# A two-way state-space block and a residual block on one core: the column chunks' sum made by an identity product and copied by ScalarE

## The chip, the core and the metric

The kernel runs on one core of a Trainium2 chip. The metric is the device time of one execution in microseconds, from the core's own clock. Names used below: PE is the tensor engine, DVE the vector engine, ACT the scalar engine, POOL the general engine, SP the engine that issues most DMAs. SBUF is the on-chip memory, PSUM the accumulation memory that PE writes.

## What is computed

The input `x` has 8 images of 64 channels and 128 by 128 points. Layer 0 runs a bidirectional selective scan along every row and, with other weights, along every column, averages the two, normalises by groups of channels and adds the input. Layer 1 is a residual block of two 3x3 convolutions with batch normalisation. Cut to what matters here:

```python
def mamba(seq, p):                       # seq: [sequences, 128, 64]
    xz = einsum('blc,ec->ble', seq, in_w)
    x, z = xz[..., :128], xz[..., 128:]
    x = silu(causal_conv(x, conv_w, conv_b))
    dt, Bm, Cm = split(einsum('bld,ed->ble', x, xp_w))
    delta = softplus(einsum('blr,dr->bld', dt, dt_w) + dt_b)
    # h = exp(delta*A)*h + delta*x*Bm ;  y = sum_n h*Cm + x*D   (16 states per channel)
    y = selective_scan(x, delta, A, Bm, Cm, D) * silu(z)
    return einsum('bld,cd->blc', y, out_w)

xr = run_bidir(rows of x, row params)    # 0.5 * (forward + reversed)
xc = run_bidir(columns of x, col params)
x_rec = 0.5 * (xr + xc)
x1 = silu(groupnorm(x_rec) * gn_w + gn_b) + x
out = relu(bn2(conv2(relu(bn1(conv1(x1))))) + x1)
```

## The kernel before

**Tiles.** An image lies in SBUF as `xt`, 128 partitions by 64 by 128: the upper 64 partitions hold the channels of the first 64 image rows, the lower 64 those of the last 64. The result of layer 0 before normalisation is gathered in `xp`, of the same shape. A unit of work, here called a group, is four rows or four columns: `N = 512` points, that is 4 sequences of 128. An image has 32 row groups (`o == 0`) and then 32 column groups (`o == 1`), so there are 512 groups in all, `n % 64` being the place of a group in its image.

**Steps.** A group has `UN = 16` steps: four groups of states, by two directions, by two halves of the channels. A step multiplies (`drive`, L367) the replicated `du` by the replicated B values, on DVE or, for the steps 2, 5, 9, 12 and 15 (`GPS`), on POOL; scans the result (`scan`, L375 or L377, DVE) with the decay factors that ACT wrote into PSUM just before (`decay`, L355 and L358, one step ahead); and multiplies by the C values (`weigh`, L382, POOL). PE sums the weighed states into `yp` every other step (`add_up`, L398) and replicates B for the DVE multiplies (`b_rows`, L347, into the single PSUM tile with tag `b`). The decay factors of the two halves have one PSUM tile each, so a decay can only start when the scan two steps before has read its tile.

**Order.** Everything is issued by hand, in the order of the loop `for s in range(total + UN)`, under a manual schedule; every engine and SP's queue run their own instructions in that order. While the steps of group `n` run, two other things are threaded in. The generator `prepare` builds group `n + 1` in thirteen pieces at the steps `PREP`: projection and short convolution (L235, L241), `u` (L266), `delta` (L275), `du` and `dl` written to a scratch in DRAM (L287 to L289), B and C (L299, `bd`), and the reads that replicate them over the partitions (L319). Its last piece, at step 13, is the gate's projection `zp` (L235 or L241, in the same PSUM tile `b`) and its ACT copy `sz` (L310). And group `n - 1` is finished: `gate` at step 3 (L405), `emit` at steps 12 and 13.

**Emission.** `emit` multiplies the gated `y` by the output weights into a PSUM tile `op` (L411), whose 128 partitions hold the 64 output channels twice. The factor 0.25 of the averages is in the weights. At the next step, a row group's result is copied by ACT into its place in `xp` (L417). A column group's result is added by DVE to what the rows left there, one addition for each half of the partitions (L422); its target view has a column's points 512 bytes apart. DVE then takes the statistics of the four finished columns (L425). After the last column group of an image, the same step collects the statistics, starts the normalisation and creates the generator of the first convolution; the pieces of both run beside the next image's row groups.

A tail follows: normalisation and first convolution of the last image, the second convolution, and the final sum. The constant `ident`, an identity of 128 by 128, is loaded for the preparation of the weights alone.

Of the kernel before, what the change touches and what calls it, by code (L numbers as in the profile page):

```python
# [9 lines left out]
F32 = mybir.dt.float32  # L10
# [5 lines left out]
P = 128  # L16
C = 64
W = 128
HH = W // 2
N = 512  # L20
SEQ = N // W
# [11 lines left out]
def tile_mamba2d_then_resblock(ctx: ExitStack, tc: tile.TileContext, x, par, gn, p_w, o_w, new_p, bn, cst, out):  # L33
    nc = tc.nc
# [12 lines left out]
    def load(shape, src, name):  # L47
        t = const.tile(shape, F32, name=name)
        nc.sync.dma_start(out=t, in_=src)
        return t  # L50
# [8 lines left out]

    fold = const.tile([P, 32], F32, name="fold")  # L60


    wt = []
    with tc.tile_pool(name="prep", bufs=2) as prep, tc.tile_pool(name="prep_ps", bufs=2, space=PSUM) as prep_ps:
        ident = prep.tile([P, P], F32, name="ident", bufs=1)
        nc.sync.dma_start(out=ident, in_=cst["ident"])
        iv = ident.rearrange("p (c n) -> p n c", n=4)
        nc.vector.tensor_add(fold, iv[:, 0, :], iv[:, 1, :])
        nc.vector.tensor_add(fold, fold, iv[:, 2, :])
# [1 line left out]
        for o, p in enumerate(par):  # L71
# [10 lines left out]
            for hf in range(2):  # L82
                h = slice(hf * C, (hf + 1) * C)
# [34 lines left out]
            wo = const.tile([P, 2, C], F32, name=f"wo{o}")  # L118
# [37 lines left out]
        for k, w in enumerate((w1, w2s)):  # L156
            nc.vector.memset(w, 0.0)
            for blk in range(2):
                for e in range(2):
                    for m in range(2):  # L160
                        kh = 2 * blk - e - m + 1
                        if 0 <= kh < 3:
                            nc.sync.dma_start(
                                out=w[e * C : (e + 1) * C, blk, :, m * C : (m + 1) * C],
                                in_=wacc[k * C : (k + 1) * C, 3 * kh : 3 * kh + 3, :],
# [37 lines left out]
    with ExitStack() as st:  # L203
# [10 lines left out]
        xp = big.tile([P, HH, W], F32, name="xp")  # L214
# [8 lines left out]
        def load_image(b):  # L223
            xb = x[b].rearrange("p (h w) -> p h w", w=W)
            RB = HH // 8
            for k in range(8):
                nc.sync.dma_start(out=xt[:, k * RB : (k + 1) * RB, :], in_=xb[:, k * RB : (k + 1) * RB, :])
# [115 lines left out]
        def b_rows(g, r):  # L343

            half, ng, d = where(r)
            pb = psa.tile([P, N], F32, name="pb", tag="b")
            nc.tensor.matmul(pb, wt[g["o"]]["wb"][:, P * ng : P * (ng + 1)], g["u"][:, d, :], start=True, stop=True)  # L347
            g["pb"] = pb

        def decay(g, r):  # L350

            half, ng, d = where(r)
            dA = g["dA", r] = psa.tile([P, 2, SEQ, W], F32, name=f"dA{half}")
            t, edge = (slice(1, W), 0) if d == 0 else (slice(0, W - 1), W - 1)
            nc.scalar.copy(dA[:, :, :, edge], zeros)  # L355
            dl = g["dl", half, d].rearrange("p q (s t) -> p q s t", t=W)
            for j in range(2):
                nc.scalar.activation(  # L358
                    dA[:, j, :, t], dl[:, j, :, t], AF.Exp, scale=wt[g["o"]]["A"][:, 2 * half + j, ng : ng + 1]
                )  # L360
# [46 lines left out]
        def emit(g):  # L407

            o, i, w = g["o"], g["i"], wt[g["o"]]
            op = psm.tile([P, 2, N], F32, name="op", tag="pt")[:, 0, :]  # L410
            nc.tensor.matmul(op, w["wo"].rearrange("p h c -> p (h c)"), g["y"], start=True, stop=True)  # L411
            yield
            o3 = op.rearrange("p (q t) -> p q t", t=W)
            if o == 0:
                hf, r = divmod(SEQ * i, HH)
                hs = slice(hf * C, (hf + 1) * C)
                nc.scalar.copy(xp[hs, r : r + SEQ, :], o3[hs])  # L417
            else:
                for hf in range(2):
                    hs = slice(hf * C, (hf + 1) * C)  # L420
                    v = xp[hs, :, SEQ * i : SEQ * (i + 1)].rearrange("p h w -> p w h")
                    nc.vector.tensor_add(v, o3[hs, :, hf * HH : (hf + 1) * HH], v)  # L422
                if i == 0:
                    stats[g["b"]] = small.tile([P, NCH, 6], F32, name="gst", bufs=1)
                nc.vector.bn_stats(stats[g["b"]][:, i, :], xp[:, :, SEQ * i : SEQ * (i + 1)])  # L425
            yield
# [76 lines left out]
        OUT = 12  # L503
# [5 lines left out]
        pieces, norm, conv3, output = (iter(()) for _ in range(4))  # L509

        def at(s):
            return gs[s // UN], s % UN

        def fetch(s):
            if s < total and s % UN in GPS:
                b_tile(*at(s))

        def fetch_c(s):
            if s < total and s % 4 == 0:
                g, r = at(s)  # L520
                c_rows(g, where(r)[1])

        def ahead(r):

            return 2 if r == GPS[0] else 3

        with tc.manual_schedule():
            load_image(0)
            for _ in prepare(gs[0], None):
                pass  # L530
            fetch_c(0)
            fetch_c(4)
            for s in range(7):
                fetch(s)
            decay(*at(0))
            b_rows(*at(0))
            drive(*at(0))
            for s in range(total + UN):
                n, r = divmod(s, UN)
                live = n < len(gs)  # L540
                prev = gs[n - 1] if n else None
                if r == 0:
                    for _ in pieces:
                        pass
                    pieces = prepare(gs[n + 1], gs[n]) if n + 1 < len(gs) else iter(())
                if s + 1 < total:
                    decay(*at(s + 1))
                    if (s + 1) % UN not in GPS:
                        drive(*at(s + 1))
                for k in (2, 3):  # L550
                    if s + k < total and (s + k) % UN in GPS and ahead((s + k) % UN) == k:
                        drive(*at(s + k))
                if live:
                    scan(*at(s))
                    weigh(*at(s))
                if r == LAG - 1 and prev:
                    gate(prev)
                if s == total - 1:
                    nc.scalar.activation(gs[n]["sz"], gs[n]["sz"], AF.Silu)
                if s % 2 == 0 and s + 2 < total:  # L560
                    b_rows(*at(s + 2))
                if r in CONV and n % PER > 5 or r >= CONV[0] and n % PER == 5:
                    next(conv3, None)
                if r in PREP:
                    next(pieces, None)
                if r == LAG and live:
                    skip(gs[n])
                if s % 2 == 0 and LAG <= s < total + LAG:
                    add_up(*at(s - LAG))
                if r in NORM and n % PER:  # L570
                    next(norm, None)
                fetch(s + 7)
                fetch_c(s + 3)
                if r == OUT and prev:
                    if n % PER == 5:
                        next(conv3, None)
                    output = emit(prev)
                    next(output)
                elif r == OUT + 1:
                    next(output, None)  # L580
                    if n % PER == 0 and prev:
                        for _ in conv3:
                            pass
                        norm = normalize(prev["b"], stats.pop(prev["b"]))
                        next(norm)
                        conv3 = conv1(prev["b"])
                elif r == 8 and live and n % PER == PER - 2 and gs[n]["b"] + 1 < B:
                    load_image(gs[n]["b"] + 1)

            for _ in range(2 * 5):  # L590
                next(norm)
            next(conv3)
            for _ in range(NT):
                for _ in range(2):
                    next(norm, None)
                for _ in range(5):
                    next(conv3)


    with ExitStack() as st:  # L600
# [15 lines left out]
        mean, r = pooled(small, [pps[:, 0:1], pps[:, 1:2]], mv, bmat, "bn1")  # L616
        s, t = affine(small, mean, r, bnp[0], bnp[1], "bn1")
# [3 lines left out]
        for k in range(2):  # L621
            xp = big.tile([P, HH + 1, W + 2], F32, name=f"xp{k}")
# [4 lines left out]
        for b in range(B):  # L627
            xp = xps[b % 2]
# [15 lines left out]
            for k in range(0, NT, 2):  # L644
                ps = psw.tile([P, 2, N], F32, name="cps")
                for j in range(2):
                    for kw in range(3):
                        for blk in range(2):
                            r = SEQ * (k + j) + blk
# [3 lines left out]
                                start=(kw == 0 and blk == 0), stop=(kw == 2 and blk == 1),  # L653
# [5 lines left out]
                hf, j0 = divmod(SEQ * k, HH // 2)  # L659
                for e in range(2):  # L660
                    nc.sync.dma_start(
                        out=c2v[hf, :, j0 : j0 + 2 * SEQ, e, :],
                        in_=cs[e * C : (e + 1) * C].rearrange("p (j w) -> p j w", w=W),
# [4 lines left out]
        mean, r = pooled(small, [pps[:, 2:3], pps[:, 3:4]], mv2, bmat, "bn2")  # L668
        s, t = affine(small, mean, r, bnp[2], bnp[3], "bn2")
# [71 lines left out]
```

## Time and profile before

| | us |
|---|---|
| median of 3 runs | 27648.13 |
| lowest and highest | 27644.12, 27659.78 |
| profiled execution, its own time | 27638.15 |
| its span | 27636.0 |
| busy DVE | 26018.6 |
| busy POOL | 25128.0 |
| busy PE | 19347.3 |
| busy ACT | 18349.8 |

The span is the time between the first and the last instruction that the profiler recorded. Busy times leave out the time in which an engine issues DMAs, branches or waits. In a group's line of the profile, the figure after the bar is the busy time in us, then the mean time of one instruction in ns, then how long the engine had been idle just before such instructions and what ended that. An fp32 product on PE stands in the records as two matrix instructions, so 512 emissions give 1024 of them. Times in the timeline are us from the start of the span; neighbouring instructions of one line are merged there, and their number is given after the x.

### The profile page before, as it was taken

The page shows a single profiled execution, that of the slowest core. Times are in us where ns is not written, and L with a number is a line of the kernel's source. Part 1 is how long each engine was busy: PE and PEld are TensorE (multiplying, and loading weights), DVE is VectorE, ACT ScalarE, POOL GpSimd, SP SyncE. Part 2 cuts the span into 40 slices and gives each one's busy share as a digit, 9 for nine tenths or more (in the row PEclk, how much of TensorE's full clock was granted, in tenths as well). Part 3 has the DMA queues.
Part 4 walks back from the last instruction along what each step waited for, and adds up shares of the span by engine and source line. Part 5 has one row for each costly group of instructions (what it writes and reads, how often), then busy time and mean ns, then how long its engine had stood idle before and what let it go on. Part 6 is the DMA issues. An engine that isn't in the chain of part 4 may idle for free.

```text
span 27636.0 us, 232983 instructions
## 1 busy us (share of the span) xinstructions
PE 19347.3 (70%) x65068; PEld 6675.0 (24%) x65068; DVE 26018.6 (94%) x16145; ACT 18349.8 (66%) x30638; POOL 25128.0 (91%) x10916
## 2 busy tenths in 40 slices
PE   6766677666776667766676667766677666776676
PEld 1222222222222222222222222222222222222222
DVE  8999999999999999999999999999999999999942
ACT  5766666666676666766667666666667666666632
POOL 7999999999999999999999999999999999999930
PEclk8888888888888888888888888888888888888888
DMA  5555555555555555555555555555555555555545
GB/s 177 173 173 173 177 183 180 173 174 178 185 175 173 172 182 185 175 173 170 183 185 173 174 176 178 184 171 176 175 185 182 170 176 176 186 176 171 172 141 188
DMA packets 1861563, 4871.45 MB, mean 176 GB/s; under 512 B 240272, under 2 KB 387872, under 8 KB 1844384
## 3 DMA queue, kind: packets, MB, share of 16 engines
q1 hardware_dynamic: 1839664, 4754.93, 52.8%
q10 hardware_dynamic: 15984, 68.06, 0.9%
q0 software_dynamic: 4608, 33.56, 0.3%
q8 instruction: 513, 8.40, 0.1%
q14 instruction: 794, 6.50, 0.1%
HBM read 4116.04 MB, written 738.98 MB: 176 GB/s over the span
## 4 chain that ended last, share of the span: by engine, by line
DVE 40%; issue 21%; PE 17%; DMA 10%; ACT 8%; POOL 2%; SPq 1%; DVEq 0%; POOLq 0%; ACTq 0%
DVE s L367 14%; DVE s L375 12%; DVE s L377 10%; DMA du<-dd 7%; PE pb L347 6%; ACT dA L358 4%; PE yp L398 3%; PE cps L650 2%; PE dp L273 2%; PE bp L295 2%; DVE du L287 2%; POOL s L382 1%; DVE y L405 1%; DMA bt<-bd 1%; PE cp L241 1%
## 5 line engine op out<-in xcount | busy, mean ns | idle before, releaser
L382 POOL TENSOR_TENSOR s<-s,c 128x1024 f32<-128x1024 f32 x8192 | 19121.0, 2364 | 1104.3 <-DMA c<-bd 440.6
L358 ACT ACTIVATE dA<-dl,A 128x508 f32<-128x508 f32 x16384 | 11274.9, 688 | 616.4 <-DMA dl<-dd 101.1
L347 PE MATMUL pb<-u,wb 128*128 128x512 f32 x8192 | 5419.6, 748 | 7657.6 <-DVE s L367 7313.1
L377 DVE TENSOR_TENSOR_SCAN s<-dA,s 128x1024 f32<-128x1024 f32 x4096 | 9296.2, 2280 | 52.3 <-ACT dA L358 40.5
L375 DVE TENSOR_TENSOR_SCAN s<-dA,s 128x1024 f32<-128x1024 f32 x4096 | 9287.2, 2278 | 0.0
L367 DVE TENSOR_TENSOR s<-du,pb 128x1024 f32<-128x1024 f32 x5632 | 6757.8, 1200 | 559.0 <-DMA du<-dd 452.1
L367 POOL TENSOR_TENSOR s<-du,bt 128x1024 f32<-128x1024 f32 x2560 | 6055.3, 2365 | 317.3 <-DMA bt<-bd 140.6
L355 ACT COPY dA<-zeros 128x8 f32<-128x8 f32 x8192 | 1349.0, 165 | 6360.6 <-DVE s L377 4676.1
L398 PE MATMUL yp<-s,fold 128*32 128x512 f32 x32768 | 5386.2, 671 | 5.3 <-POOL s L382 5.3
L347 PEld LDWEIGHTS pb<-u,wb 128*128 128x128 f32 x8192 | 1468.9, 216 | 10579.4 <-DVE s L367 5372.1
L235 PE MATMUL cp<-xt,wc 128*128 128x512 f32 (+3 forms) x4096 | 2063.2, 628 | 132.7 <-DMA xt<-x_h 76.0
L241 PE MATMUL cp<-xc,wc 128*128 128x256 f32 (+3 forms) x8192 | 2095.3, 401 | 0.0
L241 PEld LDWEIGHTS cp<-xc,wc 128*128 128x128 f32 x8192 | 1607.4, 202 | 1038.2 <-issue 459.6
L398 PEld LDWEIGHTS yp<-s,fold 128*32 128x32 f32 x32768 | 821.7, 115 | 3451.8 <-issue 2080.6
L295 PE MATMUL bp<-u,xpT 128*32 128x512 f32 x2048 | 1636.7, 948 | 4.8 <-ACT dl L289 4.8
L358 ACT ACT_TABLE_LOAD x1030 | 1321.5, 1283 | 20.3 <-DMA dl<-dd 2.3
L235 PEld LDWEIGHTS cp<-xt,wc 128*128 128x128 f32 x4096 | 782.2, 202 | 1469.4 <-issue 1116.2
L273 PE MATMUL dp<-u,wd 128*128 128x512 f32 x2048 | 1017.3, 621 | 1.2 <-ACT u L266 1.2
L299 ACT COPY bc<-bp 32x1024 f32<-32x1024 f32 x512 | 513.1, 1002 | 744.4 <-PE yp L398 677.0
L388 PE MATMUL yp<-u,dg 128*128 128x512 f32 x2048 | 961.9, 592 | 1.2 <-DVE y L405 1.2
L679 POOL DMA_DIRECT2D out<-cc x32 | 17.2, 537 | 975.6 <-ACT cc L678 975.6
L481 PE MATMUL cps<-strip,w 128*128 128x512 f32 x1536 | 754.4, 618 | 134.3 <-DMA strip<-x_d 128.0
(107 smaller groups left out, 10117.9 us busy)
## 6 DMA issues: line engine op xcount, KB each, us to landing
c<-bd SPq DMA_DIRECT2D x2049, 512.0 KB, 4.8
dl<-dd SPq DMA_DIRECT2D x2048, 512.0 KB, 6.5
du<-dd SPq DMA_DIRECT2D x2048, 512.0 KB, 7.4
bt<-bd SPq DMA_DIRECT2D x2560, 256.0 KB, 4.7
dd<-du SPq DMA_DIRECT2D x2048, 128.0 KB, 2.3
dd<-dl SPq DMA_DIRECT2D x2048, 128.0 KB, 2.4
bd<-bc SPq DMA_DIRECT2D x512, 128.0 KB, 5.4
c_d<-cs SPq DMA_DIRECT2D x256, 256.0 KB, 5.2
```

The costliest lines, as they stand in the source:

```text
L235: nc.tensor.matmul(ps[:, :, lo:hi], lhsT[hf], xt[:, r : r + SEQ, lo - s : hi - s], start=start, stop=stop)
L241: nc.tensor.matmul(ps[:, :, lo:hi], lhsT[hf], g["xc"][:, :, lo - s - hf * HH : hi - s - hf * HH], start=start and hf == 0, stop=stop and h ...
L273: nc.tensor.matmul(dp[:, d, :], w["wd"], u[:, d, :], start=True, stop=True)
L295: nc.tensor.matmul(bp[0 : 2 * NS, d, :], w["wbc"], u[:, d, :], start=True, stop=True)
L347: nc.tensor.matmul(pb, wt[g["o"]]["wb"][:, P * ng : P * (ng + 1)], g["u"][:, d, :], start=True, stop=True)
L355: nc.scalar.copy(dA[:, :, :, edge], zeros)
L358: nc.scalar.activation(dA[:, j, :, t], dl[:, j, :, t], AF.Exp, scale=wt[g["o"]]["A"][:, 2 * half + j, ng : ng + 1])
L367: engine.tensor_mul(s, g["du", half, d], b.unsqueeze(1).to_broadcast([P, 2, N]))
L375: nc.vector.tensor_tensor_scan(s, a, s, 0.0, ALU.mult, ALU.add)
L377: nc.vector.tensor_tensor_scan(s[:, ::-1], a[:, ::-1], s[:, ::-1], 0.0, ALU.mult, ALU.add)
L382: nc.gpsimd.tensor_mul(s, s, c.unsqueeze(1).to_broadcast([P, 2, N]))
L398: nc.tensor.matmul(g["yp"][32 * q : 32 * (q + 1), :], fold, s[:, j, :], start=False, stop=r == UN - 2, skip_group_check=True,)
```

## The change

The identity becomes a constant that stays in SBUF. In a column group, the output projection no longer closes its accumulation: a second product, of the identity with the stored result of the rows, goes into the same PSUM bank at step 12. That operand is read from `xp` with a column's points 512 bytes apart, and both halves of the image are read by all partitions, so that each half of the partitions finds its own columns in its own half of the bank. At step 13, two ACT copies take the place of the two DVE additions. The statistics go to step 14, after that step's scan, and with them, at the end of an image, the start of the normalisation and the creation of the convolution's generator.

```diff
+    ident = load([P, P], cst["ident"], "ident")
...
-        ident = prep.tile([P, P], F32, name="ident", bufs=1)
-        nc.sync.dma_start(out=ident, in_=cst["ident"])
...
-            nc.tensor.matmul(op, w["wo"].rearrange("p h c -> p (h c)"), g["y"], start=True, stop=True)
-            yield
+            nc.tensor.matmul(op, w["wo"].rearrange("p h c -> p (h c)"), g["y"], start=True, stop=o == 0)
             o3 = op.rearrange("p (q t) -> p q t", t=W)
+            if o == 1:
+
+                v = xp[:, :, SEQ * i : SEQ * (i + 1)].rearrange("p h w -> p w h")
+                nc.tensor.matmul(
+                    o3.rearrange("p q (f h) -> p q f h", f=2), ident, v.unsqueeze(2).to_broadcast([P, SEQ, 2, HH]),
+                    start=False, stop=True,
+                )
+            yield
...
                     v = xp[hs, :, SEQ * i : SEQ * (i + 1)].rearrange("p h w -> p w h")
-                    nc.vector.tensor_add(v, o3[hs, :, hf * HH : (hf + 1) * HH], v)
+                    nc.scalar.copy(v, o3[hs, :, hf * HH : (hf + 1) * HH])
+                yield
                 if i == 0:
...
                 elif r == OUT + 1:
                     next(output, None)
+                elif r == OUT + 2:
+                    next(output, None)
                     if n % PER == 0 and prev:
```

More of the change, by code (lines that the diff above doesn't have):

```diff
@@ L410, in emit @@
             op = psm.tile([P, 2, N], F32, name="op", tag="pt")[:, 0, :]
-            nc.tensor.matmul(op, w["wo"].rearrange("p h c -> p (h c)"), g["y"], start=True, stop=True)
+            nc.tensor.matmul(op, w["wo"].rearrange("p h c -> p (h c)"), g["y"], start=True, stop=o == 0)
+            o3 = op.rearrange("p (q t) -> p q t", t=W)
+            if o == 1:
[4 more added lines that the diff above has]
+                )
             yield
-            o3 = op.rearrange("p (q t) -> p q t", t=W)
             if o == 0:
```

## The prediction

> **What bounds the kernel now.** I read the page's engine totals first, then busy time by stretch, then DVE's waits inside those stretches, then the timeline around the edit. 0.2% of this kernel, 55 us, is about what a measurement can tell from no change.
>
> ```profile
> PE 19347.3 (70%) x65068; PEld 6675.0 (24%) x65068; DVE 26018.6 (94%) x16145; ACT 18349.8 (66%) x30638; POOL 25128.0 (91%) x10916
> ...
> L422 DVE TENSOR_TENSOR xp<-op,xp 64x256 f32<-64x256 f32 x512 | 364.0, 711 | 5.7 <-PE op L411 2.2
> L425 DVE BATCH_NORM_STATS2 gst<-xp 128x6 f32<-128x256 f32 x256 | 109.5, 428 | 8.8
> ```
>
> DVE is busy 94% of the span; the additions that go are 364 us of it. An average over stages does not say what that is worth. Taking the starts of the 512 gates (L405) as marks, I cut two stretches of image 1: eight groups that emit rows 23 to 31, free of normalisation and convolution, and 27 groups that emit columns 34 to 61. The columns of the view are PE, PEld, DVE, ACT, POOL busy, granted clock, DMA share, GB/s.
>
> ```profile
> 4651.16:5053.47 402.31, 284.03 (x927) 86.84 (x926) 393.69 (x234) 281.63 (x474) 389.63 (x169) 0.85 0.53 175
> 5204.90:6587.04 1382.14, 959.28 (x3512) 379.63 (x3511) 1378.57 (x865) 947.71 (x1593) 1317.39 (x568) 0.82 0.52 172
> ```
>
> A column group takes 1382.14 / 27 = 51.19 us and DVE is busy 1378.57 / 27 = 51.06 of them: DVE alone sets the pace there. A row group takes 402.31 / 8 = 50.29 us with DVE busy 49.21, so about 1.1 us per group are lost to waits. POOL is busy 48.7 to 48.8 us per group in both, ACT about 35, PE about 35. DVE's waits in the row stretch say what takes over when DVE has less to do:
>
> ```profile
> DVE s L367 <- DMA du<-dd: 6.7, 6, 1.7
> DVE s L367 <- PE cp L241: 1.6, 1, 1.6
> ```
>
> It is `drive(3)`, the sixth multiply after the emission, waiting for the last replicated `du`. Over the 64 such row groups I find 54 waits, mean 0.96 us over all 64, up to 2.5. In the column groups the same wait is nearly absent, because additions and statistics (1.9 us) lie ahead of it.
>
> **What the Trainium skill says.** "SBUF — State Buffer", section "Door 1", says that SBUF has 16-byte lines and that accesses going to a new line each time pay. The trace agrees: the addition at L422 handles 256 elements with a step of 512 bytes in 711 ns, while the 512-element DVE multiply at L405 takes 666; ACT's `xc` copy (L253, same step on the read) takes 624 ns for 256 elements, while a plain copy of 512 takes 586 (L310). Section "Who interferes with whom" says that a DVE instruction with one SBUF input does not hold POOL up; L422 reads one operand from PSUM, so I credit POOL with nothing. "ScalarE: Activation LUTs", section "What ACT_TABLE_LOAD costs", prices an element at 0.833 ns; 586 ns for 512 and 1005 for 1024 (L657) give 0.82.
>
> **The change part by part, for one column group.** There are 8 x 32 = 256. I use this steady one:
>
> ```profile
> 2547.33 1.13 PE L411 MATMUL op<-y,wo 128*128 128x512 f32 x2
> 2547.67 2.34 POOL L367 TENSOR_TENSOR s<-du,bt 128x1024 f32<-128x1024 f32 x1
> 2548.11 2.28 DVE L375 TENSOR_TENSOR_SCAN s<-dA,s 128x1024 f32<-128x1024 f32 x1
> 2548.24 0.73 PEld L241 LDWEIGHTS zp<-xc,wz 128*128 128x128 f32 x4 [0.61 <-DVE s L367]
> 2548.30 1.08 PE L241 MATMUL zp<-xc,wz 128*128 128x256 f32 x4
> 2549.41 0.59 ACT L310 COPY sz<-zp 128x512 f32<-128x512 f32 x1 [0.69 <-PE zp L241]
> 2549.98 7.04 POOL L382 TENSOR_TENSOR s<-s,c 128x1024 f32<-128x1024 f32 x3
> 2550.04 0.30 PEld L347 LDWEIGHTS pb<-u,wb 128*128 128x128 f32 x2 [1.08 <-ACT sz L310]
> 2550.05 1.12 PE L347 MATMUL pb<-u,wb 128*128 128x512 f32 x2 [0.68 <-ACT sz L310]
> 2550.31 1.44 DVE L422 TENSOR_TENSOR xp<-op,xp 64x256 f32<-64x256 f32 x2
> 2550.42 0.17 ACT L355 COPY dA<-zeros 128x8 f32<-128x8 f32 x1 [0.43 <-DVE s L375]
> 2550.62 1.41 ACT L358 ACTIVATE dA<-dl,A 128x508 f32<-128x508 f32 x2
> ...
> 2551.78 0.43 DVE L425 BATCH_NORM_STATS2 gst<-xp 128x6 f32<-128x256 f32 x1
> 2552.24 2.29 DVE L377 TENSOR_TENSOR_SCAN s<-dA,s 128x1024 f32<-128x1024 f32 x1
> ```
>
> 1. **Removed:** two additions. From their start to the statistics' start is 2551.78 - 2550.31 = 1.47 us of DVE, all on the bounding engine. The floor of a column group becomes 51.19 - 1.47 = 49.72 us.
>
> 2. **Added on PE:** one identity product, two records like L411 (1024 for 512 emissions). Plain, two passes hold the queue at most 2548.24 - 2547.33 = 0.91 us. The operand steps by 512 bytes, which no matmul here shows: lower end 0.9 (hidden by PE's own rate), upper end 0.9 x 2.2 = 2.0, the ratio by which the stepped L422 and L253 exceed 256 plain elements (711 against 666 - 0.5 x (1200 - 666) = 399 ns; 624 against 586 - 0.5 x (1005 - 586) = 377). I take 1.4. Behind it on PE stand `zp` and then `b_rows` for the next group.
>
> 3. **Added on ACT:** two 64x256 copies with a stepped write. Lower end 0.38 us each (the plain value just worked out), upper end 0.71 (what DVE needed for the same place); I take 0.62 from L253. As no load of an activation table stands ahead of L310, none is added. They queue behind the `sz` copy, hence behind `zp`, hence behind the identity product. Behind them on ACT is the decay for the scan of step 15 (0.17 + 1.41 us), and, on DVE, the statistics wait for them.
>
> 4. **Moved:** the statistics go from after scan 13 to after scan 14. Without the additions scan 14 starts at 2550.31 and ends about 2552.5: that scan is the cover. With m for the product and c for a copy, PE reaches `zp` at about 2547.33 + 0.91 + m, `zp` takes 1.1, `sz` 0.65 with its wait, so the copies end at 2549.99 + m + 2c. The overrun is X = max(0, m + 2c - 2.5). My values give 2.64, X about 0.15; plain ones give none; stepped throughout (2.0 and 0.71) 0.9. Early in a column stage `zp` starts later: 1830.76 with the additions at 1832.25, 1.49 us ahead, where the group above has 2.01 (2548.30 and 2550.31). There X is 0.65 with my values and 1.4 at the top. Over all groups I take 0.4. `b_rows` of step 16 ends 2.9 us after `zp`'s start (1.1 + 0.65 + 1.12), about 2552.5, ahead of its multiply at 2553.1; the delayed decay ends about 2554.2, when statistics (0.46) and that multiply (1.12) are just through. Neither adds a second wait, but the decay has nothing to spare.
>
> 5. **Late next:** `du`. SP issues its last replicas after the landing of `bd`, which hangs on ACT's `bc` copy of step 11, ahead of all edits, so they land where they did. DVE arrives 1.47 us earlier, less X. A row group has neither additions nor statistics (0.46), so its 64 waits, each shortened by 0.46 + 0.4, are my estimate: mean 0.35 us. Bounds: 0.04 (an arrival like the columns') to 0.6 (X nil).
>
> 6. **Once an image:** normalisation starts one step later, eight times; its aggregation, two pooling products, some dozen small DVE operations and its square root move along, while its DMAs still start with the next group. Same DVE work, and decays and scans surround it at either step: nothing, with 10 us either way as bound. The constant's larger life and one DMA moved ahead of the weight preparation: under 1 us. No other DMA changes place, and POOL issues nothing new; its 48.8 us still fit.
>
> Sum: 49.72 + 0.4 + 0.35 = 50.47, a saving of 0.72 us; x 256 = 184 us, some of it not had in the first groups of a stage: **170 us**. The profiled execution took 27638.15 (span 27636.0), the median of the runs shown is 27648.13; against the median the forecast is **27478 us**.
>
> **The rivals.**
> A, the forecast (0.48): some overrun and some `du` wait, saving 90 to 230 us.
> B (0.27): cover holds, reads and writes are near plain speed, and `du` comes as early as in the columns: 1.47 - 0.3 = 1.17 us, 300 us saved, 27348. For it: one scan is 2.28 us against a chain of 1.7 to 2.6. Against: the row groups' waits.
> C (0.13): the chain takes it back. X of 1.1 plus 0.25 of `du` leaves 0.1 us per group, some 28 us: 27620. For it: the stepped operand on both engines.
> D, slower (0.12): the step costs PE more than it costs DVE and ACT. Place: PE's queue at step 12, with `zp`, `sz`, copies and the decay of scan 15 strung behind it. It decides from m + 2c = 2.5 + 1.47 = 4.0 us, that is m above 2.7 with c at 0.62. At m = 3.5, X is 2.24, `du` no longer waits, and the group is 0.77 us longer: 197 us, 27845. Against it: nothing on two engines paid over 2.2 times. That the copies don't free DVE at all is excluded: the additions are gone from its queue.
>
> **The numbers.** Faster 0.75 (A and B), same 0.13, slower 0.12. Low end 27340 (all of B); high end 27620, which takes in C and leaves out D.
>
> **What would show it.** Right: ACT copies into `xp` of about 0.62 us, the column stretch at 50.5 us per group, waits of some tenths ahead of the statistics on these copies, and `du` waits as in the row groups. Wrong: an identity product over 2 us, a group over 51.2 us, or scan 15 waiting for its decay. A POOL that idles less than 0.3 us per group would mean I took the wrong next bound.

## The result, and the profile after

The changed kernel takes 27504.62 us (median of 6 runs, 27472.73 to 27526.96) against 27651.19 us (6 runs) for the kernel before: a ratio of 0.9946, 95% interval 0.9933 to 0.9959, or 147 us less. The forecast was 27478 us, with bounds of 27340 and 27620. The profiled execution took 27504.13 us, its span 27502.4.

On the page of the changed kernel, the engine totals: DVE is busy 341 us less, PE 365 and ACT 257 us more.

```profile
PE 19712.6 (72%) x65580; PEld 6745.5 (25%) x65580; DVE 25677.6 (93%) x15633; ACT 18606.5 (68%) x31150; POOL 25117.1 (91%) x10916
```

The groups of instructions of the changed kernel that the diff made. The identity product is L416, the copies are L429, the statistics L433:

```profile
L416 PE MATMUL op<-xp,ident 128*128 128x512 f32 x512 | 480.5, 1027 | 0.0
L429 ACT COPY xp<-op 64x256 f32<-64x256 f32 x512 | 307.0, 600 | 16.9 <-PE op L416 13.9
L433 DVE BATCH_NORM_STATS2 gst<-xp 128x6 f32<-128x256 f32 x256 | 107.4, 420 | 99.7 <-ACT xp L429 98.5
```

A copy takes 600 ns. The statistics, which waited 8.8 us in all before, now wait 99.7, nearly all for the copies. The same two stretches of image 1 as before, by busy time (PE, PEld, DVE, ACT, POOL, clock, DMA share, GB/s):

```profile
4628.52:5029.13 400.61, 282.57 (x927) 86.19 (x926) 393.57 (x233) 281.64 (x474) 389.54 (x169) 0.86 0.54 176
5179.25:6544.18 1364.93, 990.42 (x3566) 378.45 (x3565) 1341.12 (x811) 975.24 (x1647) 1315.74 (x568) 0.87 0.53 174
```

The row groups are where they were (400.61 / 8 = 50.08 us). A column group takes 1364.93 / 27 = 50.55 us, of which DVE is busy 49.67. It is no longer busy all the time, and its waits in that column stretch say for what:

```profile
DVE gst L433 <- ACT xp L429: 10.6, 17, 0.8
DVE s L367 <- DMA du<-dd: 10.4, 15, 1.3
DVE s L367 <- PE pb L347: 1.5, 5, 0.3
```

Two new waits of nearly the same size, 0.39 us per group each: one for the copies, one for the replicated `du`. One emission in the timeline shows how the first arises:

```profile
9410.50 1.13 PE L411 MATMUL op<-y,wo 128*128 128x512 f32 x2
9410.75 2.28 DVE L375 TENSOR_TENSOR_SCAN s<-dA,s 128x1024 f32<-128x1024 f32 x1
9411.47 1.88 PE L416 MATMUL op<-xp,ident 128*128 128x512 f32 x2
9412.95 2.27 DVE L377 TENSOR_TENSOR_SCAN s<-dA,s 128x1024 f32<-128x1024 f32 x1
...
9413.17 1.04 PE L241 MATMUL zp<-xc,wz 128*128 128x256 f32 x4
...
9414.25 0.58 ACT L310 COPY sz<-zp 128x512 f32<-128x512 f32 x1 [2.87 <-PE zp L241]
...
9414.73 1.21 ACT L429 COPY xp<-op 64x256 f32<-64x256 f32 x2
9414.88 1.13 PE L347 MATMUL pb<-u,wb 128*128 128x512 f32 x2 [0.68 <-ACT sz L310]
...
9415.96 0.43 DVE L433 BATCH_NORM_STATS2 gst<-xp 128x6 f32<-128x256 f32 x1 [0.74 <-ACT xp L429]
```

The identity product holds PE's queue from 9411.47 to 9413.17, 1.70 us. `zp`, `sz` and the copies follow one after the other, and the statistics, which need the copies, start 0.74 us after scan 14 has ended (9412.95 + 2.27 = 9415.22, against 9415.96).

To compare kernels I averaged period and DVE waits from the traces over the same 27 column groups of all 8 images (216 groups), in us per group. "Rows" is the period of the undisturbed row groups 23 to 31. The kernels e1 to e11 are explained below.

| kernel | time (median) | rows | column group | wait for copies | for B rows | for du |
|---|---|---|---|---|---|---|
| before | 27651 | 50.21 | 51.23 | none | 0.01 | 0.06 |
| changed | 27505 | 50.37 | 50.61 | 0.37 | 0.06 | 0.46 |
| e1, plain operand | 27456 | 50.30 | 50.39 | 0.00 | 0.03 | 0.78 |
| e2, no identity product | 27446 | 50.20 | 50.35 | 0.00 | 0.03 | 0.76 |
| e3, copies and statistics later | 27514 | 50.31 | 50.56 | 0.00 | 0.49 | 0.44 |
| e11, product later too | 27403 | 50.38 | 50.26 | 0.00 | 0.05 | 0.62 |
| e5, before with the later B tile | 27301 | 49.49 | 51.17 | none | 0.00 | 0.00 |
| e4, changed with the later B tile | 27027 | 49.56 | 50.15 | 0.40 | 0.03 | 0.00 |
| e9, e11 with the later B tile | 26921 | 49.39 | 49.67 | 0.00 | 0.04 | 0.00 |
| e10, e9 with the tile at step 12 | 26829 | 49.18 | 49.51 | 0.00 | 0.00 | 0.01 |
| e6, before with the statistics later | 27646 | 50.16 | 51.20 | none | 0.10 | 0.09 |
| e7, changed with the copies on DVE | 27632 | 50.19 | 51.20 | none | 0.15 | 0.08 |

### The profile page after: what moved, and what is told of

It is laid out like the page before. It is cut to its first block, busy times and chain, and to the rows that moved or that the text cites. A ratio compares the mean times of both kernels' runs of the same rounds, so it can differ in the third digit from the quotient of the medians.

```text
span 27502.4 us, 234256 instructions
## 1 busy us (share of the span) xinstructions
PE 19712.6 (72%) x65580; PEld 6745.5 (25%) x65580; DVE 25677.6 (93%) x15633; ACT 18606.5 (68%) x31150; POOL 25117.1 (91%) x10916
## 5 line engine op out<-in xcount | busy, mean ns | idle before, releaser
L382 POOL TENSOR_TENSOR s<-s,c 128x1024 f32<-128x1024 f32 x8192 | 19109.1, 2365 | 906.3 <-DMA c<-bd 419.2
L367 POOL TENSOR_TENSOR s<-du,bt 128x1024 f32<-128x1024 f32 x2560 | 6053.5, 2365 | 375.4 <-DMA bt<-bd 138.1
```

The lines of the kernel that those rows point to most:

```text
L367: engine.tensor_mul(s, g["du", half, d], b.unsqueeze(1).to_broadcast([P, 2, N]))
L382: nc.gpsimd.tensor_mul(s, s, c.unsqueeze(1).to_broadcast([P, 2, N]))
```

## The experiments

The theory under test: the change offers 1.47 us of DVE per column group, and two things take more than half of it back. The stepped operand makes the identity product long, and what stands behind it on PE is late; and `du`, which was hidden by the additions, arrives too late for a faster DVE. The main rivals: that the copies are late for ACT's own sake, and that transfer time rather than issue order makes `du` late.

**e1: a product with a plain operand.** The rows' result of these columns is left out.

```diff
-                v = xp[:, :, SEQ * i : SEQ * (i + 1)].rearrange("p h w -> p w h")
+                v = xp.rearrange("p h w -> p (h w)")[:, 2 * P * i : 2 * P * (i + 1)].rearrange("p (w h) -> p w h", h=HH)
```

> The identity product reads 256 neighbouring points of xp in place of the stepped columns, so it adds other points than the rows' result of these columns; all else is as in the changed kernel. Theory (the stepped operand makes the product 1.70 us long, and with it zp, sz and the two copies late): the product falls to about 0.9 us, the wait of the statistics for the copies falls from 0.37 us per column group to under 0.1, the wait for du rises from 0.46 to 0.6, and the column group goes from 50.6 to about 50.3 us, some 70 us less in all, 27435. Rival (the two copies behind sz are late whatever the product takes): the wait of the statistics stays at 0.3 to 0.4 and the time stays within 30 us of the changed kernel's 27505.

The product's records in this kernel (minimum, median, maximum of one record in ns):

```profile
L416 PE MATMUL op<-xp,ident x512: 592/592/593, 1833.8 to 26331.9; 128*128 128x512 f32 x171
```

The record falls from 1034 to 592 ns, the wait for the copies disappears, and the time is 27456.26 us (ratio 0.9928, 0.9915 to 0.9940): the stepped operand is the cause of that wait. Of the 0.37 us, 0.32 came back as `du` wait, more than the 0.14 expected. The ratio's interval overlaps that of the changed kernel, so here the waits carry the verdict, not the time.

**e2: no identity product.** The rows' result is not added.

```diff
-            nc.tensor.matmul(op, ..., start=True, stop=o == 0)
+            nc.tensor.matmul(op, ..., start=True, stop=True)
...
-            if o == 1:
-                ...
-                nc.tensor.matmul(... ident, v.unsqueeze(2).to_broadcast([P, SEQ, 2, HH]), start=False, stop=True)
```

> The identity product is left out, so the rows' result is not added; the ACT copies and the moved statistics stay. Theory (du is late next, and takes what the cover gives): no wait of the statistics for the copies, a du wait of about 0.6 us per column group, 50.3 us per group and 27435 in all, no better than with a plain operand although PE has 1.7 us less to do. Rival (PE's queue itself still costs, through the replicated B rows of step 16): clearly below the plain operand, by 0.3 us per group or more, under 27370.

27445.68 us (0.9925, 0.9912 to 0.9937), 50.35 us per group: like e1 within what can be told. As far as these runs can tell, a plain product would be free at this place: what leaves the wait for the copies goes to the wait for `du`, now 0.76 us, so relieving PE further gained nothing.

**e3: copies and statistics one step later.**

```diff
             else:
+                yield
                 for hf in range(2):
...
                 elif r == OUT + 2:
                     next(output, None)
+                elif r == OUT + 3:
+                    next(output, None)
```

> The changed kernel with the column copies at step 14, behind that step's decay on ACT, and the statistics at step 15, behind its scan. Theory (the copies are late only against the end of scan 14): the statistics wait for nothing, the du wait rises to about 0.6 us, the group is 50.3 us, 27435 in all. Rival (the copies' 1.2 us on ACT are late at any place, now before the decay of the scan of step 16, or the wait is only passed on to du in full): a scan waits for its decay by 0.3 us or du takes all of it, 50.6 us per group, 27505 within 30.

27513.91 us (0.9949, 0.9937 to 0.9962): the rival's time, by a wait that neither expectation named. DVE's waits in the column stretch of image 1:

```profile
DVE s L367 <- PE pb L347: 13.4, 24, 0.8
DVE s L367 <- DMA du<-dd: 13.0, 15, 2.1
```

The multiply of step 16 now waits for its B rows (0.49 us per group). These stand behind `zp` and `sz` as the copies do, so they are late for the same product; in the changed kernel the wait for the copies came first and covered it. Moving what waits does not help while what is late stays.

**e11: the product itself moved,** behind the B rows of step 16 on PE, with copies and statistics at step 15.

```diff
-            if o == 1:
-                v = ...; nc.tensor.matmul(... ident ...)
             yield
+            if o == 1:
+                yield
+                v = ...; nc.tensor.matmul(... ident ...)
+                yield
...
-                yield
                 if i == 0:
...
+                elif r == OUT + 3:
+                    next(output, None)
```

> The changed kernel with the product at step 14 and copies and statistics at step 15, with the DMA order left as it was. Theory (du catches whatever DVE gains before it): no waits for copies or B rows around the emission, a du wait of 0.75 us per column group as with the plain operand and without the product, 50.35 us per group, 27445 in all. Rival (the two waits are independent, so that removing one keeps the other at 0.46): 50.0 us per group, 27370 or below.

27403.19 us (0.9913, 0.9899 to 0.9926). Both waits around the emission are gone, and `du` takes 0.62 us, less than the 0.75 expected but far from independent of the rest. The time lies between the two expectations, 42 us below the first. It is also 42 us below e2, which has no product at all; a difference of 0.15% is too small to read anything into.

**e4: the B tile that waits for `bd` issued behind the replicas.** The tile of the next group's step 2 goes from seven steps ahead to five.

```diff
-            if s < total and s % UN in GPS:
-                b_tile(*at(s))
+            for k in (5, 7):
+                if s + k < total and (s + k) % UN in GPS and ((s + k) % UN == GPS[0]) == (k == 5):
+                    b_tile(*at(s + k))
...
-                fetch(s + 7)
+                fetch(s)
```

> The changed kernel with one DMA issued later: the B tile of the next group's step 2, which must wait for the landing of bd, is issued at step 13 after the last replicas of dl and du, not at step 11 ahead of the last two pairs. Theory (du is late because its issue stands in SP's queue behind that tile): the du waits mostly go, in row groups (0.95 us) and column groups (0.46 us) alike, and if the total of 534 us of du waits halves the time falls by 250 us or so, to about 27250; the column group is near 50.2 us. Rival (the transfers themselves, 512 KB each at some 7 us to landing, are the limit, or POOL now waits for the B tile): du waits stay near 0.4 and 0.9 us, or POOL's wait for bt appears, and the time is 27500 or above.

27026.91 us, a ratio of 0.9773 (0.9759 to 0.9786): 478 us below the changed kernel, nearly twice the expected gain, and hardly a `du` wait left in columns (0.00 us per group) or undisturbed rows (0.02). SP's queue in the changed kernel, from the write of `bd` to the last replica (start, duration):

```profile
9408.37 0.32 SPq L301 DMA_DIRECT2D bd<-bc  x1
...
9413.04 0.51 SPq L340 DMA_DIRECT2D bt<-bd  x1
9413.59 0.60 SPq L319 DMA_DIRECT2D dl<-dd  x1
9414.30 0.55 SPq L319 DMA_DIRECT2D du<-dd  x1
9414.94 0.55 SPq L319 DMA_DIRECT2D dl<-dd  x1
9415.58 0.69 SPq L319 DMA_DIRECT2D du<-dd  x1
```

and the same in e4:

```profile
9267.70 0.32 SPq L301 DMA_DIRECT2D bd<-bc  x1
...
9271.54 0.51 SPq L319 DMA_DIRECT2D dl<-dd  x1
9272.31 0.51 SPq L319 DMA_DIRECT2D du<-dd  x1
9273.50 0.51 SPq L340 DMA_DIRECT2D bt<-bd  x1
```

The tile needs `bd` to have landed; until then it holds up two pairs of replicas that don't. Without it in front, the last `du` is here issued 4.61 us after the write of `bd` instead of 7.21. What SP's queue waited at the tiles for the landing of `bd`, over the whole of the changed kernel and then of e4 (us in total, times, longest):

```profile
SPq L340 <- DMA bd<-bc: 1991.8, 511, 6.2
SPq L340 <- DMA bd<-bc: 269.8, 342, 2.8
```

The rival of a slow transfer is ruled out by the landings. Over the 216 column groups, the last `du` is issued 4.4 us after the write of `bd` in e4 and 8.1 in the changed kernel. It then takes longer to land, 9.4 us against 8.7, and yet lands 2.9 us earlier. The rival's other sign did appear: POOL's waits for the tile grew from 138 to 477 us in all, and through them DVE waits 0.31 us per undisturbed row group and 0.04 per column group for POOL.

**e5: the same move on the kernel before.** The edit is that of e4.

> The kernel before, with only the B tile's DMA of the next group's step 2 issued at step 13 in place of step 11. Theory (the change loses part of its 1.47 us per column group to du, which a late issue causes): row groups gain as they did on top of the change (from 50.3 to 49.6 us), column groups stay at 51.1 to 51.2 us because they had no du waits; 27330 in all, so that the change is worth about 1.0 us per column group, some 280 us in all, on top of this one against 150 without it. Rival (the issue order acts on all groups alike): the column groups fall too and the difference to the changed kernel with the same order stays near 150 us, 27180.

27300.89 us (0.9875, 0.9860 to 0.9890), 350 us below the kernel before. Rows gain, columns stay at 51.17 us. Freed of `du`, the change is worth 27301 - 27027 = 274 us (1.02 us per column group in place of 0.62).

**e6: the move of the statistics alone,** in the kernel before: a `yield` ahead of the statistics, and the branch for step 14.

> The kernel before with the statistics, and once an image the start of the normalisation, one step later; the DVE additions stay where they were. Theory (the move costs nothing by itself): 27650 within 30 us, column groups at 51.2 us. Rival (the pooling at the end of an image waits longer at step 14): 10 us per image more in the last column group, 27700 or above.

27646.40 us, a ratio of 0.9999 (0.9991 to 1.0007). The move costs nothing that the time shows.

**e7: DVE makes the copies.**

```diff
-                    nc.scalar.copy(v, o3[hs, :, hf * HH : (hf + 1) * HH])
+                    nc.vector.tensor_copy(v, o3[hs, :, hf * HH : (hf + 1) * HH])
```

> The changed kernel with DVE making the two copies in place of ACT, at the same step 13. Theory (the gain is the DVE time handed to ACT, and the identity product only costs): two DVE copies of 0.4 to 0.7 us each stand on the bounding engine, and the product makes zp and with it the B rows of step 16 late; a column group of 50.8 to 51.3 us, 27560 to 27680 in all, close to the kernel before. Rival (a copy on DVE is as good as one on ACT, since its own wait disappears): 27505 within 30 us.

The copies' records:

```profile
L429 DVE COPY xp<-op x512: 565/600/616, 1826.1 to 26492.0; 64x256 f32<-64x256 f32 x171
```

27632.31 us (0.9996, 0.9988 to 1.0004). A copy on DVE takes 600 ns, as on ACT, against 711 for the addition; the wait for the B rows of 0.15 us per group takes most of what that leaves. With DVE as the writer, the sum in PSUM gains nothing that can be told: the gain is that ACT, not DVE, writes it.

**e9: e11 and e4 together.**

> The changed kernel with the later B tile DMA, and with the identity product issued at step 14, behind the B rows of step 16 on PE, and copies and statistics at step 15. Theory (what stalls DVE is the 1.7 us product ahead of zp and of those B rows, not the copies): no wait for the B rows and at most 0.1 us for the copies, column groups at 49.8 us against 50.15 with the later DMA alone, 90 us less than its 27027, about 26940. Rival (the copies on ACT are late wherever they stand): the statistics wait 0.3 us or more at step 15, column groups stay at 50.1 us, 27030 within 20.

26921.18 us (0.9738, 0.9725 to 0.9751). The column stretch of image 1:

```profile
5086.91:6425.31 1338.40, 993.61 (x3566) 376.81 (x3565) 1335.80 (x812) 982.88 (x1647) 1315.88 (x568) 0.86 0.52 178
```

1338.40 / 27 = 49.57 us per group, DVE busy 49.47: it is all but back to back again. What DVE still waits for in the columns is POOL, 0.12 us per group over all images. Against e5, averaged over all images, the column group is 51.17 - 49.67 = 1.50 us shorter: the whole of the 1.47 that the removed additions took.

**e10: the tile at step 12,** between the last two pairs: `(6, 7)` and `k == 6` in the edit of e4.

> As the version with the later product and the later B tile, but this tile is issued one step earlier, at step 12, between the last two pairs of replicas. Theory (at step 13 the tile comes a little late for POOL, which shows as 0.5 to 0.8 us per group of waits for bt, of which DVE feels 0.1 to 0.7): POOL's waits for bt shrink, DVE's waits for POOL go, 26880 in all. Rival (the tile's wait for the landing of bd holds up the last pair of du again): du waits of 0.3 us per group or more come back, 26980 or above.

26828.93 us, a ratio of 0.9705 (0.9692 to 0.9719), some 50 us below the expectation and 676 below the changed kernel. DVE's waits for POOL are gone from the undisturbed groups; POOL's waits for the tile are back to 146 us in all, from 522 in e9. Of the `du` waits, 0.38 us per group came back in the row groups 5 to 15, which run beside normalisation and convolution, and about 0.01 elsewhere: the tile holds up one pair instead of two, and the last `du` is issued 6.9 us after the write of `bd` in the column groups, between the 4.6 of e9 and the 8.1 of the changed kernel. This version beats both kernels.

## Why the prediction was right, point by point

- **What bounds.** DVE's 51.19 us per column group, with 1.47 of it removed: right. With both waits out of the way, e9 against e5 recovers 1.50.
- **The product.** Taken as 1.4 us between bounds of 0.9 and 2.0; it holds the queue for 1.70. The stepped operand doubles a pass. This term was too small by 0.3 us. The factor of 2.2 for its upper end is not the ratio of the whole instructions that stands beside it, which is 1.8 (711 / 399) on DVE and 1.7 (624 / 377) on ACT; it comes out when the part that does not grow with the elements (132 ns on DVE, 167 on ACT, by the same figures) is taken off both.
- **The copies.** Taken as 0.62 us, measured 0.60. No activation table is loaded for them.
- **The overrun.** With the measured values the prediction's formula gives 1.70 + 1.20 - 2.5 = 0.40, or 0.30 with the cover of 2.6 us that its own lines give (scan 14 would end at 2550.31 + 2.29 = 2552.60, not 2552.5). The statistics wait 0.37 us, where the sum took 0.4. That agreement is luck: the extra half microsecond for early groups, which made up for the short product in that figure, is not there (0.40 us over the first five column groups of an image, 0.37 in the steady ones). The two errors cancelled.
- **"Neither adds a second wait."** True of the decay. Of the B rows it held only because the wait for the copies comes first: DVE waits 0.06 us for them in the changed kernel, and 0.49 in e3 when that wait is out of the way.
- **`du` late next.** Right in kind and in cause: the last replicas are issued after the landing of `bd`, as e4 showed by moving what waits for it. The size was 0.35 and is 0.46 us. The estimate shortened the row groups' waits by everything that DVE does or waits for more than a row group, yet e1 shows that nearly all of a removed wait returns here.
- **Moved work and the end of an image.** Nothing was expected, with 10 us either way. In the changed kernel the interval between the last gate of an image and the first of the next is 0.7 us longer (56.5 against 55.8), 5 us in all. In the traces of e6, e7 and e4, which have the move as well, it is 56.5, 56.0 and 55.7, so nothing can be read from it, and e6's time shows nothing. POOL, credited with nothing, gained nothing: its multiplies (L382) take 2365 ns where they took 2364.
- **The sum.** 50.47 us per group was forecast, 50.61 measured. Averaged over all images, a group is 0.62 us shorter where 0.72 was forecast, and the `du` wait, 0.46 for 0.35, is about that difference. For the whole kernel: 184 us before the rounding for early groups, 170 after, 147 measured. In the traces the column groups give 153 us; the tail after the last gate is 17 us longer in this profile (1138.7 against 1121.5), which no edit explains: in the experiments, where the tail's code is the same, it lies between 1125 and 1140.

Rival B failed on both its conditions, the plain operand and the early `du`; e9 against e5 shows that its 1.17 us per column group could be had and passed, but only with the product moved and SP's queue reordered. C and D needed X of 1.1 and 2.2 us; it was 0.37.

## What to carry to other kernels

Work taken off the bounding engine is worth its time only until the next arrival: list what that engine will reach earlier, and look at stages that already run at the new pace, as the row groups did here. A step that leaves one engine and passes through others puts its longest link ahead of everything queued behind it there; moving the link (e11) helped where moving the waiter (e3) did not. And in a queue that issues in order, a transfer that waits for a landing belongs behind those that don't, but no later than its own reader allows, as e10 showed with another 92 us over e9. The move of e4 was worth 478 us on top of the change and 350 us without it, where the change itself gave 147.

## What the runs showed of the hardware that was not expected

Reading an fp32 operand with a step of 512 bytes costs PE twice the queue time: its two records start 0.84 us apart against 0.43 in e1 (medians; one record takes 1034 against 592 ns). Copying 64x256 from PSUM into such steps takes 600 ns on DVE (e7) and on ACT alike, about as long as ACT's plain copy of twice as many elements (580 ns, L424).
